# Next pair's rows prepared in DRAM during the second scan, stores spread over the convolution's start, and the quarter-size convolution's loads issued by GpSimd

## The chip, the core and the metric

One core of a Trainium2 chip runs the whole kernel. Its engines are TensorE (PE, with weight loads listed as PEld), VectorE (DVE), ScalarE (ACT), GpSimd (POOL) and SyncE (SP, which here only issues transfers). Each engine works through its own instructions in order; transfers (DMAs) are issued by SP, ACT or POOL and run on 16 shared DMA engines. The metric is device time of one execution in microseconds (us): less is better. The time given for a kernel is the median of its runs.

## The reference

Eight images of 64 channels and 128 x 128 pixels in float32 pass four residual layers, each of which adds its output to its input. Every layer reads a group norm of the image. Cut to what matters:

```python
x = x + relu(batchnorm(deform_conv2d(gn(x), offset, mask, wd)))   # layer 0: 3x3 deformable convolution
x = x + conv3x3(gn(x), weight)                                    # layer 1
v = gn(x)                                                         # layer 2: two state space scans
y_h = s5_block(v.transpose(0, 2, 3, 1), 0)                        #   along rows of the image
y_v = s5_block(v.transpose(0, 3, 2, 1), 1)                        #   along columns
x = x + fusion_w @ concat(y_h, y_v) + fusion_b
v = gn(x)                                                         # layer 3: nearest neighbours
x1 = relu(bn(conv2d(v, wd, stride=4)))                            #   64 x 32 x 32, quarter size
out = mean over the 9 least similar of a 7x7 window(x1) - x1
f = relu(bn(conv3x3(concat(x1, out)))); f = f * sigmoid(bn(wa @ mean(f)))
x = x + bilinear_resize(f, 128, 128)
```

A group norm has 32 groups of two channels and takes its statistics over a whole image, so each layer's first step waits for the last pixel of the layer before. The batch norm of layer 0 takes its statistics over all eight images: its output y is kept in DRAM until all are done, and normalised later.

## The kernel before

**Tiling.** The 128 partitions hold 2 images x 64 channels, a *pair*; four pairs p = 0 to 3 make the batch. A pair is 128 x 16,384 floats, 8 MB.

**Stages.** `deform` makes layer 0 without its batch norm for all pairs and leaves y[p] in DRAM. It takes the first 14.0 ms, and the change does not reach it. `rest` (from L477) does everything else. It owns two *rooms* in SBUF, each as large as a pair: one holds the current pair's image `a`, the other, `b`, holds what the step needs beside it. For each pair:

1. `conv3x3` (layer 1). The statistics of its group norm, `gn1`, come from the routine that made the image. Sixteen times it normalises 8 rows of the image on ACT (nx, L574) and copies them with four transfers on SP into the other room (L576, L577), whose first and middle rows POOL clears first. Then 16 groups of 4 row pairs run: two sets of matmuls (c1, L588), a DVE add onto the image (L590), two DVE statistics (L594).
2. `scan_layer` (layer 2). A first norm fills `b`; then two `Scan` objects, d = 0 along rows and d = 1 along columns. Each goes backward over 16 blocks (`back`, which leaves states in DRAM) and then forward (`ahead`), in steps g. A step of `ahead` has: `inputs` (ACT, fx, L1224, read from `b`; four transfers in<-fx on SP, L1226), `drive` (PE, L1235, then v and u, the sum u on POOL at L1242), `scan` (DVE, L1257), `rebuilt` (one transfer zb<-back on SP, L1280, PE L1282, POOL L1286 and L1288), `outputs` (PE L1302, ACT, DVE L1305), `mixed` (PE L1320, ACT), and `add` of the block before (POOL L1334, PE L1338, DVE add onto the image L1340, and for d = 1 a DVE statistic L1343).
3. The finished image is stored to y[p] with 16 transfers of 512 KB, all issued at once on SP (L504). The room `a` is then the other room for the next pair, and its clearing waits for these stores.
4. `neighbours` (layer 3) is a generator named `aside`. It is not run here: the next pair's `conv3x3` takes one step of it after each set of matmuls, so that layer 3 of pair p lies inside layer 1 of pair p + 1. For the last pair it runs alone at the end. Its first part, `quarter` (L1002), loads weights (L1014), the norm's numbers (L1016) and then, in 8 blocks of 4 transfers each, the image (yq, L1036; from y[p] in DRAM, or from the room for the last pair), all issued by ACT; it runs matmuls pd (L1044) and an activation x1q (L1045). After it come the nine least similar (`farthest`, DVE), their means, a convolution pf (L1112), and the resize, which loads y[p] again (L1135), adds on DVE (L1151, L1152) and stores the output.

**The work around the change.** During the second scan's `ahead`, a generator `following` is stepped once per step g. In the kernel before it does nothing 15 times; at the end, when `b` is no longer needed, it runs `finish_deform` for pair p + 1 into `b`: 16 rows, each a load of x into `b` (L540), a load of y (L542), a batch norm and relu on ACT (L543), an add (L544, on POOL and DVE in turn) and two DVE statistics (L546). Then `gn1` is made from the statistics. y has three buffers in turn, taken from tiles that the scan has finished with.

A scheduler orders the instructions of an engine, within what buffers and data allow; the program's order is therefore not exactly an engine's order.

Of the kernel before, what the change touches and what calls it, by code (L numbers as in the profile page):

```python
# [9 lines left out]
F32 = mybir.dt.float32  # L10
I32 = mybir.dt.int32
AF = mybir.ActivationFunctionType
# [4 lines left out]
P = 128  # L17
# [3 lines left out]
CH = 512  # L21
NCH = HW // CH
# [6 lines left out]
NB = 256  # L29
NG = HW // (T * NB)  # L30

MAT, COS, SIN, ROT, DEC = 0, T * P, T * P + NB + 1, T * P + 2 * NB + 2, T * P + 2 * NB + 2 + P
NSTATE = DEC + 1
# [8 lines left out]
class Net:  # L42
# [434 lines left out]
    def rest(self):  # L477
        tc, nc = self.tc, self.nc
        with ExitStack() as ctx:
            pool = lambda name, bufs, **kw: ctx.enter_context(tc.tile_pool(name=name, bufs=bufs, **kw))  # L480
            self.big = pool("b_big", 1)
            self.small = pool("b_small", 2)
            self.tables = pool("b_tables", 2)
            self.ps = pool("b_ps", 2, space=PSUM)
            self.ps1 = pool("b_ps1", 1, space=PSUM)
            self.back = [[self.dram.tile([P, 2, NB], F32, name=f"back{d}_{g}") for g in range(NG)] for d in range(2)]
            rooms = [self.big.tile([P, ROOM], F32, name=f"room{k}") for k in range(2)]
            image = lambda t: t[:, 0:HW].rearrange("p (h w) -> p h w", h=H)
            aside = iter(())
            with tc.tile_pool(name="b_first", bufs=6) as wp:  # L490
                first = self.finish_deform(0, image(rooms[0]), lambda n: wp.tile([P, 1024], F32, tag="y", name=f"yr0_{n}"))
                for _ in first:
                    pass
            for p in range(self.npair):
                now, other = rooms[p % 2], rooms[(p + 1) % 2]
                a, b = image(now), image(other)
                r, nb = self.conv3x3(p, a, other, *self.gn1, aside)
                norm = self.scan_layer(p, a, b, r, nb)
                af = now[:, 0:HW]

                for n in range(8):
                    for half in range(2):
                        s = slice((half * 8 + n) * 1024, (half * 8 + n + 1) * 1024)
                        nc.sync.dma_start(self.y[p][:, s], af[:, s])  # L504
                aside = self.neighbours(p, self.y[p] if p + 1 < self.npair else af, norm)
            for _ in aside:
                pass

    def setup_deform(self, psum):

# [36 lines left out]
            yield  # L547
        self.gn1 = self.groupnorm(self.small, self.ps1, "small", st, "gn1")

    def conv3x3(self, p, a, room, r, nb, aside):  # L550

        nc, src = self.nc, self.ins["l1_w"]
        st = self.small.tile([P, NCH, 6], F32, tag="st", name=f"gn2_st{p}")
        two = room.rearrange("p (i n w) -> p i n w", i=2, w=H)
        half = [slice(0, C), slice(C, P)]
        with self.tc.tile_pool(name=f"b_conv{p}", bufs=1) as cp, self.tc.tile_pool(name=f"b_conv2_{p}", bufs=2) as wp:

            w = cp.tile([P, 2, 2, 3, C], F32, name=f"l1_w{p}")
            nc.gpsimd.memset(w, 0.0)
            for e in range(2):
                for n in range(2):
                    for h in range(2):
                        dy = 2 * n - 1 + h - e
                        if abs(dy) < 2:
                            nc.scalar.dma_start(w[half[h], e, n], src[:, 3 * dy + 3 : 3 * dy + 6, :])
            nc.gpsimd.memset(two[half[0], :, 0, :], 0.0)
            nc.gpsimd.memset(two[half[1], :, H // 2, :], 0.0)  # L570
            for n in range(16):
                t = wp.tile([P, 2, 4, H], F32, tag="t", name=f"nx{p}_{n}")
                rows = a[:, 8 * n : 8 * n + 8, :].rearrange("p (m e) w -> p e m w", e=2)
                nc.scalar.activation(t, rows, AF.Identity, bias=nb, scale=r)  # L574
                for i in range(2):
                    nc.sync.dma_start(two[half[1], i, 4 * n : 4 * n + 4, :], t[half[i], 0])  # L576
                    nc.sync.dma_start(two[half[0], i, 4 * n + 1 : 4 * n + 5, :], t[half[i], 1])  # L577
            for n in range(0, H // 2, 4):
                for e in range(2):
                    po = self.ps.tile([P, 4, H], F32, tag="b", name=f"c1_{p}_{n}_{e}")  # L580
                    calls = []
                    for dx in (0, -1, 1):
                        c0, c1 = max(0, -dx), min(H, H - dx)
                        for m in range(2):
                            for i in range(2):
                                calls.append((po[half[i], :, c0:c1], w[:, e, m, dx + 1], two[:, i, n + m : n + m + 4, c0 + dx : c1 + dx]))
                    for k, (o, lt, mv) in enumerate(calls):
                        nc.tensor.matmul(o, lhsT=lt, rhs=mv, start=k < 2, stop=k >= len(calls) - 2)  # L588
                    rows = a[:, 2 * n : 2 * n + 8, :].rearrange("p (m e) w -> p e m w", e=2)[:, e]
                    nc.vector.tensor_add(rows, rows, po)  # L590
                    next(aside, None)
                for k in range(2):
                    g = n // 2 + k
                    nc.vector.bn_stats(st[:, g, :], a[:, 4 * g : 4 * g + 4, :].rearrange("p h w -> p (h w)"))  # L594
                next(aside, None)
            for _ in aside:
                pass
        return self.groupnorm(self.small, self.ps1, "small", st, "gn2")
# [319 lines left out]
    def scan_layer(self, p, a, b, r, nb):  # L918

        tc, nc = self.tc, self.nc  # L920
        st = self.small.tile([P, NCH, 6], F32, tag="st", name=f"gn3_st{p}")
        with tc.tile_pool(name=f"b_scan{p}", bufs=2) as wp:
            ways = [Scan(self, wp, p, d, a, b, st) for d in range(2)]

            back = ways[0].back("in", "z", "h")
            for _ in self.first_norm(wp, p, a, b, r, nb):
                next(back)
                next(back)
            for _ in back:
                pass  # L930
            ways[0].ahead(ways[1].back("inb", "zbk", "fx"))

            def following():

                rooms = [(wp, "inb", [P, 2, 2, NB]), (wp, "fx", [P, 2, 2, NB]), (self.tables, "tabs", [P, NSTATE])]

                def room(n):
                    pool, tag, shape = rooms[n % 3]
                    kind = {"bufs": 1} if pool is wp else {}
                    t = pool.tile(shape, F32, tag=tag, name=f"yr{p + 1}_{n}", **kind)  # L940
                    return t[:, 0:1024] if len(shape) == 2 else t.rearrange("p i h m -> p (i h m)")

                for _ in range(NG - 1):
                    yield
                for n, _ in enumerate(self.finish_deform(p + 1, b, room)):
                    if n % 4 == 3:
                        yield

            ways[1].ahead(following() if p + 1 < self.npair else iter(()))

        r, nb = self.groupnorm(self.small, self.ps1, "small", st, "gn3")
        nc.vector.scalar_tensor_tensor(nb, self.bias, r, nb, ALU.mult, ALU.add)
        norm = self.small.tile([P, 2], F32, tag="norm", name=f"norm{p}")
        nc.vector.tensor_copy(norm[:, 0:1], r)
        nc.vector.tensor_copy(norm[:, 1:2], nb)
        return norm
# [45 lines left out]
    def quarter(self, sp, p, src, norm, x1):  # L1002


        nc, S = self.nc, self.S
        half = [slice(0, C), slice(C, P)]
        with self.tc.tile_pool(name=f"b_down{p}", bufs=1) as wp, self.tc.tile_pool(name=f"b_down2_{p}", bufs=3) as yp:
            wd = wp.tile([P, 2, 4, C], F32, name=f"l3_wd{p}")
            taps = self.ins["l3_wd"].rearrange("c (m e g) o -> c e m g o", m=2, e=2)

            norms = wp.tile([P, 2, 2], F32, name=f"norms{p}")
            for e in range(2):
                for m in range(2):
                    nc.scalar.dma_start(wd[half[e], m], taps[:, e, m])  # L1014
                for i in range(2):
                    nc.scalar.dma_start(norms[half[e], i], norm[half[i]])  # L1016
            wd = wd.rearrange("p m g o -> p (m g) o")

            pb = self.ps1.tile([P, 1], F32, tag="small", name=f"pb{p}")
# [11 lines left out]
            for n in range(-2, 8):  # L1031
                if n + 2 < 8:
                    y = yp.tile([P, 2, 8, H], F32, tag="y", name=f"yq{p}_{n + 2}")
                    for e in range(2):
                        for i in range(2):
                            nc.scalar.dma_start(y[half[e], i], rows[half[i], e, 8 * n + 16 : 8 * n + 24, :])  # L1036
                    loaded.append(y)
                if n < 0:
                    continue
# [383 lines left out]
```

## Time and profile before

| what | us |
|---|---|
| median of 4 runs | 18606.06 |
| lowest, highest run | 18596.14, 18632.25 |
| profiled execution, its own time | 18649.83 |
| its span (what the page shows) | 18648.1 |
| PE busy | 11167.3 (60%) |
| DVE busy | 11385.0 (61%) |
| POOL busy | 11000.9 (59%) |
| ACT busy | 3026.1 (16%) |
| start of `rest` in the span | 13,986 |

The page shows one execution. A busy share is a mean over stages with different limits: the deformable stage has 75% of the span. The change is in `rest`, so its stages have to be read one by one, from windows of the trace. The end chain that the page prints covers only the last microseconds and tells nothing of the middle. The mean granted TensorE clock of the execution is 0.76.

In the answers of the trace, a line of a group reads: source line, engine, operation, out<-in, shapes, count | busy us, mean ns of one | idle time of the engine just before them and what ended it. A timeline line reads: start us, length us, engine, line, operation. "SPq" is SP's queue: the time it spends issuing a transfer.

### The profile page before, as it was taken

The page shows a single profiled execution, that of the slowest core. Times are in us where ns is not written, and L with a number is a line of the kernel's source. Part 1 is how long each engine was busy: PE and PEld are TensorE (multiplying, and loading weights), DVE is VectorE, ACT ScalarE, POOL GpSimd, SP SyncE. Part 2 cuts the span into 40 slices and gives each one's busy share as a digit, 9 for nine tenths or more (in the row PEclk, how much of TensorE's full clock was granted, in tenths as well). Part 3 has the DMA queues.
Part 4 walks back from the last instruction along what each step waited for, and adds up shares of the span by engine and source line. Part 5 has one row for each costly group of instructions (what it writes and reads, how often), then busy time and mean ns, then how long its engine had stood idle before and what let it go on. Part 6 is the DMA issues. An engine that isn't in the chain of part 4 may idle for free. (4 is left out here: it accounts for less than half of the span.)

```text
span 18648.1 us, 118301 instructions
## 1 busy us (share of the span) xinstructions
PE 11167.3 (60%) x31224; PEld 3939.1 (21%) x31224; DVE 11385.0 (61%) x27180; ACT 3026.1 (16%) x5658; POOL 11000.9 (59%) x10484
## 2 busy tenths in 40 slices
PE   6555455545555554555645555554427988889886
PEld 1111111111111111111111111111102534435343
DVE  5566666566665566665655665555664765667566
ACT  1000111001100000110000000000003424334242
POOL 5667676676666667666666666666671413315142
PEclk8777677767677676777766766667658999999898
DMA  4333333333333333333333333333333243422433
GB/s 152 101 96 106 115 116 113 109 118 114 115 109 98 97 95 117 116 111 111 100 97 91 97 100 96 97 96 95 89 92 95 68 144 78 129 87 72 140 77 99
DMA packets 900049, 1933.33 MB, mean 104 GB/s; under 512 B 199852, under 2 KB 435764, under 8 KB 876340
## 3 DMA queue, kind: packets, MB, share of 16 engines
q0 software_dynamic: 442368, 1208.55, 22.2%
q1 hardware_dynamic: 381968, 679.49, 12.0%
q10 hardware_dynamic: 75044, 37.72, 1.0%
q8 instruction: 255, 4.18, 0.1%
q14 instruction: 414, 3.39, 0.1%
HBM read 1540.72 MB, written 208.10 MB: 94 GB/s over the span
## 5 line engine op out<-in xcount | busy, mean ns | idle before, releaser
L371 POOL DMA_INDIRECT g<-table,idx x9216 | 9526.6, 1034 | 4321.7 <-issue 2636.6
L381 DVE TENSOR_REDUCE sm<-g 128x64 f32<-128x256 f32 x9216 | 5065.9, 580 | 3567.8 <-remote 2744.1
L289 PE MATMUL po<-xe,wt 128*54 128x512 f32 (+3 forms) x8384 | 4720.6, 673 | 772.3 <-ACT ob L299 545.1
L380 DVE TENSOR_TENSOR g<-g,wts 128x256 f32<-128x256 f32 x9216 | 3558.8, 415 | 562.3 <-DMA g<-table,idx 476.1
L387 PE MATMUL sp<-ident,sm 128*128 128x128 f32 x4096 | 1498.9, 377 | 3483.7 <-DVE sm L381 1833.0
L390 ACT COPY s<-sp 128x512 f32<-128x512 f32 x1024 | 599.1, 585 | 9514.4 <-remote 3935.2
L387 PEld LDWEIGHTS sp<-ident,sm 128*128 128x128 f32 x4096 | 620.5, 155 | 6261.9 <-DVE sm L381 2391.3
L395 PE MATMUL yp<-s,wd 128*64 128x512 f32 (+1 forms) x2560 | 911.5, 719 | 1351.9 <-ACT s L390 733.5
L289 PEld LDWEIGHTS po<-xe,wt 128*54 128x54 f32 x8384 | 922.3, 139 | 2115.7 <-issue 1294.9
L872 POOL COPY l_yb<-ln_y 128x512 f32<-128x512 f32 x128 | 73.1, 615 | 1295.8 <-DVE ln_y L121 1295.8
L588 PE MATMUL c<-room,l_w 128*64 128x508 f32 (+1 forms) x3072 | 740.1, 597 | 21.3 <-DMA room<-nx 15.2
L1242 POOL TENSOR_TENSOR u<-u,v 128x512 f32<-128x512 f32 x256 | 328.5, 1283 | 689.5 <-DVE v L1241 552.7
L1224 ACT ACTIVATE fx<-room,ln_b,ln_g 128x512 f32<-128x512 f32 x512 | 639.2, 1292 | 169.4 <-DMA in<-fx 147.7
L1334 POOL TENSOR_TENSOR ms<-ms,ln_y 128x512 f32<-128x512 f32 x256 | 274.3, 1092 | 638.9 <-DVE ln_y L121 602.7
L389 PE MATMUL s<-ident,sm 128*64 128x128 f32 x1024 | 344.3, 336 | 431.7 <-DVE g L380 110.1
L395 PEld LDWEIGHTS yp<-s,wd 128*64 128x64 f32 (+1 forms) x2560 | 221.0, 158 | 1773.7 <-issue 985.0
L1257 DVE TENSOR_TENSOR_SCAN z<-tabs,z,u 128x256 f32<-128x256 f32 x512 | 434.6, 875 | 215.1 <-POOL u L1242 186.5
L1235 PE MATMUL pv<-in,tabs 128*128 128x512 f32 x1024 | 506.7, 617 | 44.5 <-DVE u L1241 41.2
L396 DVE BATCH_NORM_STATS2 ystat<-yp 128x6 f32<-128x512 f32 x128 | 89.2, 697 | 706.4 <-PE yp L395 413.5
L1320 PE MATMUL pc<-outs,h 128*128 128x256 f32 x2048 | 496.7, 385 | 26.2 <-DVE h L1305 23.9
L1302 PE MATMUL py<-x,outs 128*128 128x512 f32 x1024 | 508.0, 600 | 7.2 <-POOL x L1288 6.8
L1302 PE MATMUL py<-in,outs 128*128 128x512 f32 x1024 | 507.5, 608 | 3.3 <-DMA outs<-out_tab 1.8
(414 smaller groups left out, 10216.7 us busy)
## 6 DMA issues: line engine op xcount, KB each, us to landing
g<-table,idx POOLq DMA_INDIRECT x9216
in<-fx SPq DMA_DIRECT2D x1024, 128.0 KB
xe<-in_x_dram SPq DMA_DIRECT2D x56, 1408.0 KB
table<-q SPq DMA_DIRECT2D x256, 256.0 KB
y<-ys SPq DMA_DIRECT2D x128, 256.0 KB
room<-in_x_dram SPq DMA_DIRECT2D x64, 512.0 KB
yr<-y SPq DMA_DIRECT2D x64, 512.0 KB
room<-nx SPq DMA_DIRECT2D x256, 128.0 KB
```

The source lines that it names most:

```text
L289: nc.tensor.matmul(po[:, r0:r1, c0:c1], lhsT=wt[:, t, :], rhs=xe[:, row + r0 : row + r1, c0 + dx : c1 + dx], start=n == 0, stop=n == len(u ...
L371: nc.gpsimd.indirect_dma_start(out=tq[:, k, :], out_offset=None, in_=flat[i], in_offset=bass.IndirectOffsetOnAxis(ap=idx[:, at : at + 1], ...
L380: nc.vector.tensor_mul(t[:, k], t[:, k], w)
L381: nc.vector.tensor_reduce(sm[:, k], t[:, k].rearrange("p q c -> p c q"), axis=mybir.AxisListType.X, op=ALU.add)
L387: nc.tensor.transpose(sp[:, j, :], sm[:, j * P : (j + 1) * P], self.ident)
L390: nc.scalar.copy(st[i][:, 0:4, m * P : (m + 1) * P], sp)
L395: nc.tensor.matmul(yp[i * C : (i + 1) * C, :], lhsT=wd[0:rows, j, :], rhs=st[i][0:rows, j, :], start=j == 0, stop=j == 4)
L588: nc.tensor.matmul(o, lhsT=lt, rhs=mv, start=k < 2, stop=k >= len(calls) - 2)
L1224: nc.scalar.activation(fx[:, e].rearrange("p h (o m) -> p h o m", m=self.INNER), src[:, e::2], AF.Identity, bias=w["ln1_b"], scale=w["ln1_g"])
L1235: nc.tensor.matmul(pv, lhsT=tabs[:, at : at + P], rhs=fx[:, :, h, :], start=h == 0, stop=h == 1)
L1302: nc.tensor.matmul(py, lhsT=lt, rhs=mv, start=n == 0, stop=n == len(calls) - 1)
L1320: nc.tensor.matmul(pc[:, i], lhsT=hs[:, h, i, m * P : (m + 1) * P], rhs=self.outs[:, CEN : MIX + P], start=True, stop=True)
```

## The change

Three things are changed, all in `rest`.

1. `following` runs a new routine, `prepare_deform`, in the steps that were empty. For each of the 16 rows of pair p + 1 it loads x and y into two SBUF tiles (one buffer each), normalises y on ACT, adds on POOL (always), takes two statistics on DVE, and stores the sum back into y[p + 1] in DRAM. It takes `gn1` from these statistics at once. When `b` is free, eight transfers of 1 MB load the finished image from y[p + 1] into it. The first pair still uses `finish_deform`.
2. The 16 stores of y[p] become a generator, `stores`, of 8 steps with two transfers each. `conv3x3` of the next pair takes two steps before the rooms are cleared and one after every second nx. For the last pair all 16 are issued before `neighbours`, as before.
3. The weight, norm and image loads of `quarter` (40 transfers per pair) are issued by GpSimd instead of ACT.

```diff
@@ rest
-            aside = iter(())
+            aside, stores = iter(()), iter(())
...
-                r, nb = self.conv3x3(p, a, other, *self.gn1, aside)
+                r, nb = self.conv3x3(p, a, other, *self.gn1, stores, aside)
                 norm = self.scan_layer(p, a, b, r, nb)
                 af = now[:, 0:HW]
-
-                for n in range(8):
-                    for half in range(2):
-                        s = slice((half * 8 + n) * 1024, (half * 8 + n + 1) * 1024)
-                        nc.sync.dma_start(self.y[p][:, s], af[:, s])
+                stores = self.stores(p, af)
                 aside = self.neighbours(p, self.y[p] if p + 1 < self.npair else af, norm)
+            for _ in stores:
+                pass
             for _ in aside:
                 pass
+
+    def stores(self, p, af):
+
+        for n in range(8):
+            for half in range(2):
+                s = slice((half * 8 + n) * 1024, (half * 8 + n + 1) * 1024)
+                self.nc.sync.dma_start(self.y[p][:, s], af[:, s])
+            yield
@@ new
+    def prepare_deform(self, p, xr, yr):
+
+        nc = self.nc
+        st = self.small.tile([P, NCH, 6], F32, tag="st", name=f"gn1_st{p}")
+        for n in range(16):
+            s = slice(n * 1024, (n + 1) * 1024)
+            nc.sync.dma_start(xr, self.x[p * P : (p + 1) * P, s])
+            nc.sync.dma_start(yr, self.y[p][:, s])
+            nc.scalar.activation(yr, yr, AF.Relu, bias=self.bn0_bias, scale=self.bn0_scale)
+            nc.gpsimd.tensor_add(xr, xr, yr)
+            for m in range(2):
+                nc.vector.bn_stats(st[:, 2 * n + m, :], xr[:, m * CH : (m + 1) * CH])
+            nc.sync.dma_start(self.y[p][:, s], xr)
+            yield
+        self.gn1 = self.groupnorm(self.small, self.ps1, "small", st, "gn1")
@@ conv3x3
+            for _ in range(2):
+                next(stores, None)
             nc.gpsimd.memset(two[half[0], :, 0, :], 0.0)
             nc.gpsimd.memset(two[half[1], :, H // 2, :], 0.0)
             for n in range(16):
...
+                if n % 2:
+                    next(stores, None)
@@ scan_layer, following
-                rooms = [(wp, "inb", [P, 2, 2, NB]), (wp, "fx", [P, 2, 2, NB]), (self.tables, "tabs", [P, NSTATE])]
...
+                xr = wp.tile([P, 2, 2, NB], F32, tag="inb", name=f"xr{p + 1}", bufs=1).rearrange("p i h m -> p (i h m)")
+                yr = self.tables.tile([P, NSTATE], F32, tag="tabs", name=f"yr{p + 1}")[:, 0:1024]
+                made = self.prepare_deform(p + 1, xr, yr)
                 for _ in range(NG - 1):
+                    next(made, None)
                     yield
-                for n, _ in enumerate(self.finish_deform(p + 1, b, room)):
-                    if n % 4 == 3:
+                for _ in made:
+                    pass
+
+                bf = b.rearrange("p h w -> p (h w)")
+                for n in range(8):
+                    s = slice(n * 2048, (n + 1) * 2048)
+                    nc.sync.dma_start(bf[:, s], self.y[p + 1][:, s])
+                    if n % 3 == 2:
                         yield
@@ quarter
-                    nc.scalar.dma_start(wd[half[e], m], taps[:, e, m])
+                    nc.gpsimd.dma_start(wd[half[e], m], taps[:, e, m])
...
-                    nc.scalar.dma_start(norms[half[e], i], norm[half[i]])
+                    nc.gpsimd.dma_start(norms[half[e], i], norm[half[i]])
...
-                            nc.scalar.dma_start(y[half[e], i], rows[half[i], e, 8 * n + 16 : 8 * n + 24, :])
+                            nc.gpsimd.dma_start(y[half[e], i], rows[half[i], e, 8 * n + 16 : 8 * n + 24, :])
```

More of the change, by code (lines that the diff above doesn't have):

```diff
@@ L548, in finish_deform, with conv3x3 @@
         self.gn1 = self.groupnorm(self.small, self.ps1, "small", st, "gn1")
-    def conv3x3(self, p, a, room, r, nb, aside):
+    def prepare_deform(self, p, xr, yr):
[12 more added lines that the diff above has]
+        self.gn1 = self.groupnorm(self.small, self.ps1, "small", st, "gn1")
+    def conv3x3(self, p, a, room, r, nb, stores, aside):
         nc, src = self.nc, self.ins["l1_w"]
@@ L933, in following @@
             def following():
-                rooms = [(wp, "inb", [P, 2, 2, NB]), (wp, "fx", [P, 2, 2, NB]), (self.tables, "tabs", [P, NSTATE])]
[L937 to L941, printed above, removed]
+                xr = wp.tile([P, 2, 2, NB], F32, tag="inb", name=f"xr{p + 1}", bufs=1).rearrange("p i h m -> p (i h m)")
+                yr = self.tables.tile([P, NSTATE], F32, tag="tabs", name=f"yr{p + 1}")[:, 0:1024]
+                made = self.prepare_deform(p + 1, xr, yr)
                 for _ in range(NG - 1):
+                    next(made, None)
                     yield
-                for n, _ in enumerate(self.finish_deform(p + 1, b, room)):
-                    if n % 4 == 3:
+                for _ in made:
[5 more added lines that the diff above has]
+                    if n % 3 == 2:
                         yield
```

## The prediction

> **What bounds the kernel now.** I read the busy time by slice first: up to 14.0 ms PE, DVE and POOL share the deformable stage, which this change leaves as it is. The last 4,662 us (13,986 to 18,648) hold four pairs, and only there can time move. Next came windows: the second scan's steady stretch of pair 0, then the tail of each pair's second scan, from its last input (L1224) to its last statistic (L1343). Columns: window, length, busy PE, PEld, DVE, ACT, POOL, granted clock, DMA share, GB/s.
>
> ```profile
> 14800.00:14957.10 157.10, 156.96 (x519) 89.35 (x518) 139.75 (x291) 68.98 (x140) 87.85 (x70) 1.00 0.20 50
> 14959.99:15051.50 91.51, 53.01 (x152) 29.52 (x152) 82.18 (x144) 30.81 (x49) 48.17 (x29) 0.78 0.60 201
> 16093.70:16184.60 90.90, 54.33 (x155) 29.93 (x153) 82.58 (x146) 30.96 (x49) 49.08 (x30) 0.76 0.59 200
> 17225.90:17315.60 89.70, 53.27 (x154) 29.47 (x153) 82.72 (x147) 30.84 (x49) 48.56 (x30) 0.77 0.60 202
> 18355.30:18412.30 57.00, 45.21 (x154) 25.85 (x152) 46.03 (x105) 15.07 (x35) 24.15 (x21) 0.90 0.07 18
> ```
>
> The steady scan is PE-bound (156.96 of 157.10), with DVE close behind (13.97 of 15.71 us a step). The tail of pairs 0 to 2 carries the next pair's 16 rows and is DVE-bound; pair 3 has no next pair and shows the bare tail.
>
> ```profile
> L546 DVE BATCH_NORM_STATS2 gn_st<-room 128x6 f32<-128x512 f32 x32 | 21.3, 680 | 2.7 <-POOL room L544 2.7
> L544 POOL TENSOR_TENSOR room<-room,yr 128x1024 f32<-128x1024 f32 x8 | 19.4, 2429 | 14.1 <-ACT yr L543 12.5 <-DMA room<-in_x_dram 1.6
> L543 ACT ACTIVATE yr<-yr,bn_bias,bn_scale 128x1024 f32<-128x1024 f32 x14 | 17.4, 1245 | 11.6 <-DMA yr<-y 11.5
> L544 DVE TENSOR_TENSOR room<-room,yr 128x1024 f32<-128x1024 f32 x8 | 12.5, 1566 | 0.0
> ```
>
> These groups of the first tail are the rows: 33.8 us of DVE explain 82.18 against 46.03. Then SP's timeline in the steady steps (start, length, instruction):
>
> ```profile
> 14921.65 0.33 SPq L1280 DMA_DIRECT2D zb<-back  x1
> 14923.19 2.38 SPq L1226 DMA_DIRECT2D in<-fx  x4
> 14937.37 0.33 SPq L1280 DMA_DIRECT2D zb<-back  x1
> 14938.91 2.38 SPq L1226 DMA_DIRECT2D in<-fx  x4
> 14953.08 0.33 SPq L1280 DMA_DIRECT2D zb<-back  x1
> 14954.63 3.50 SPq L1226 DMA_DIRECT2D in<-fx  x4
> ```
>
> A step is 15.71 us and SP must issue four in<-fx in each. The last set goes at 14954.63 and the matmul that reads it, L1235, starts at 14960.02 after 0.32 us of waiting for it: there is no spare time behind these loads. Last, the waits of the stage after, conv of pair 1 with pair 0's quarter convolution:
>
> ```profile
> DVE room L590 <- PE c L588: 100.5, 17, 35.9
> ...
> ACT nx L574 <- DMA room<-nx: 41.6, 12, 7.9
> ...
> ACT x1q L1045 <- DMA yq<-y: 25.4, 1, 25.4
> ACT nx L574 <- DVE gn_nb L149: 21.4, 1, 21.4
> ```
>
> With T = 15,048 (last add, L1340): the stores go at 15,048.96, gn1 is ready at 15,057.2, ACT issues twelve yq from 15,061.97 for 23.06 us between two nx, the first c1 starts at T+42.
>
> **Part 1: rows out of the tail.** The tail falls from a mean of 90.70 to 57.00: **-33.7 us** a pair, three times. Below 57 it can't go: the last steps' own chain sets that, as in pair 3.
>
> **Part 2: rows into the scan.** In the built order of the changed program SP holds, between the in<-fx of one step and of the next, one or two rows of: store (waits for POOL's add), yr load, xr load (waits until that store has landed, xr being single). Sixteen rows fall in nine steps: seven of two, two of one. Steps of before: 9 x 15.71 = 141. Length of one row, r:
> - Store, issue to landing. The nearest row is nx's 128 KB, 2.47 us (pair 0: last issue at 14,042.63, ACT released at 14,045.10). A further 384 KB at 366 GB/s (the window of 15,050 to 15,060, when y's stores run) is 1.1: 3.5 (an estimate). The yr load beside it, another 512 KB or 1.4: up to 5.0. I take 4.2.
> - xr load, alone: 3.5. POOL add 2.35 (L544's undisturbed instances; the mean is 2.43, the longest 3.16). Issue of the second DMA 0.35. Waiting in POOL's queue, busy 8.8 of 15.7 us a step already: 0 to 0.8, I take 0.4.
> So r = 10.8, from 9.6 to 12.0. SP runs in order, so in<-fx stands behind both rows: from the xr issued just before one in<-fx to that before the next lie two whole rows, and a step with two lasts 2r. After a one-row step, xr and the add have already run while SP waited, and it is 3.9 (in and zb issues) + (r - 6.25: without 3.5 + 2.35 + 0.4) + r. A one-row step stays 15.71. Sum: 5 x 21.6 + 2 x 19.25 + 2 x 15.71 = 178, **+37 us** a pair; 161 (+20) at 9.6, 195 (+53) at 12.0. The other queues follow in the same time: PE waits at L1235, and everything behind it in PE's order, scan and outputs, with it. DVE gets two statistics (2 x 0.68) per row and, in a two-row step, needs 13.97 + 2.7 = 16.7 of 21; POOL 8.8 + 4.9; ACT 6.9 + 2.5: these are covered by the longer step, and without it DVE alone would need 13.97 + 16 x 1.36 / 9 = 16.4 a step, 6 us over nine.
>
> The Trainium skill ("SBUF — State Buffer", section "Who interferes with whom") says that a DVE instruction with two SBUF inputs and a GpSimd one that reads SBUF exclude each other for a whole instruction, which speaks against adds on POOL alone. The trace leans the same way: at 14,970.00, beside a POOL add (14,969.92, 2.34 us), two scans of L1257 took 4.41 us on DVE, against a mean of 0.875 each. By the rule, 16 x 2.35 = 38 us would be taken from DVE where such instructions meet; spread over nine steps that is 4.2 each, and the two-row step would be near 21 on DVE too, so not a second price but the same one.
>
> **Part 3: b filled by eight 1 MB loads.** 8 MB at 366 GB/s is 23 us and lies in the bare tail of 57, whose DMA share is 0.07. Three of them stand on SP ahead of the last in<-fx, which shares its engines with them: 0 to 8 (3 x 2.9), I take **+3**.
>
> **Part 4: stores in conv, gn1 early, quarter off ACT.** Conv starts sooner: two store steps instead of eight, no gn1 wait, no yq between nx. Memsets wait about 5 us for stores (15,048.96 to 15,053.99 before), nx and room<-nx take 5: first c1 at about T+11, not T+42. But DVE's chain ends the stage. Before: last pd at T+105, then x1 18, farthest 70, means and pf 17, to up 25, up 60, next stage 8: 304, as measured. In the built order the eighth pd moves from behind c1_12_1 to behind c1_24_1: 11 + 6.75 groups x 10.94 (conv of pair 0: 175 us for 16 groups) + 8 pd x 4 = T+117, 12 later; gn2's chain, now inside up, gives back 7. **+5 us** a pair. Bounds: -30 (the earlier start is kept: pd does not hold the chain) to +15.
>
> **Part 5: 40 loads per pair issued by POOL.** Before shows no plain POOL load; the nearest row is
>
> ```profile
> L371 POOL DMA_INDIRECT g<-table,idx x9216 | 9526.6, 1034 | 4321.7 <-issue 2636.6
> ```
>
> with 128 pieces of data an instruction; a yq load has 64 x 8 rows of 512 B, so 0.95 (its median) to 4 x 0.95 = 3.8. I take 2.1, nearer the row, since the row is the only instance of a POOL issue. In conv, four of 2.1 are 8.4 against 10.94 per group: hidden by PE. At the end of the program nothing hides them:
>
> ```profile
> 18412.70:18484.00 71.30, 40.53 (x299) 28.63 (x299) 5.45 (x27) 3.67 (x8) 0.00 (x0) 0.75 0.96 235
> ```
>
> Here the 16 DMA engines are at 0.96, so a cheaper issue gains nothing: 40 x 2.1 = 84 against 71, **+13**, from 0 to 152 - 71 = +81. The skill ("SBUF — State Buffer", section "SBUF: two separate sides") warns that DVE can keep GpSimd from writing descriptors, and gives 3,100 ns where one takes 620 alone. By that figure 40 would be 124, an estimate of +53; but DVE is busy 5.45 of 71.3 us here.
>
> **Sum**: 3 x (-33.7 + 37 + 3 + 5) + 13 = **+47**. The profiled execution took 18,649.8 (span 18,648.1 and 1.7 outside), so 18,697 by its own time; that execution lies 43.8 above the median of 18,606, against which I forecast **18,653**.
>
> **Rivals.**
> - *The rows fit* (faster): if r is at its lower end, 9.6, they cost 20, and if conv keeps 20 of its 31 us, 3 x (-33.7 + 20 + 3 - 20) = -92 and the quarter 0: **18,514**. For it: DVE and POOL have room, DMA share is 0.20. Against: in<-fx behind the rows, and DVE's up chain. With the rest as taken, the sign turns at rows of 21 us, r = 9.7.
> - *A draw*: rows 28 (r = 10.2), conv -5, quarter 0: 3 x (-7.7) = -23, **18,583**. Same mechanism, smaller rows.
> - *POOL's issue is the bound*: at 3.8 a yq block takes 15.2, more than a conv group (the point where it decides is 10.94/4 = 2.7). Then pd ends 15 later, 3 x (11.3 + 15) + 81 = +160, **18,766**. For it: 512 pieces per load. Against: L371's 1.03 mean with DVE busy 61%.
> - *The scheduler leaves the rows in the tail*: excluded by the built order.
>
> **Numbers.** Forecast 0.48, the rows fit 0.24, draw 0.18, POOL's issue 0.10. The forecast's own range is 18,610 to 18,710 (rows 28 to 46, quarter 0 to 35). About 0.2%, 37 us, can be told from no change. Slower: 0.40 of the forecast and POOL's 0.10, 0.50; within: 0.08 and 0.16, 0.24; faster: 0.24 and 0.02, 0.26. For 8 in 10 the range reaches down to the better part of the first rival and up short of the third: 18,530 to 18,745.
>
> **What would show it.** Tails of 57 to 62 us in pairs 0 to 2; second-scan steps of 19 to 22 us alternating with 15.7, with PE waiting at L1235's matmul for in<-fx, SP at the store and at xr; first c1 near T+11 but the next stage near T+304 to 310; POOL issue rows of about 2 us. Wrong if the steps stay at 15.7 (rows free), if the tail keeps 90, if c1's earlier start reaches the next stage, or if x1q waits for yq in every group.

## The result and the profile after

The changed kernel takes 18,666.89 us (median of 49 runs) against 18,608.46 us (75 runs): ratio 1.0026, with a 95% interval of 1.0018 to 1.0035, so about 48 us slower (the two medians lie 58 apart). The forecast was +47. Its sum came out, but not all of its terms, and the reason given for the largest of them fell.

The profiled execution of the changed kernel has a span of 18,686.4 us, 38.3 more than before. To see where they lie I cut the span into stages at marks that every kernel has: a *scan stage* runs from a pair's first centring matmul (L902 before, L928 after) to the last statistic of its second scan (L1343, L1371), a *convolution stage* from there to the next pair's first centring matmul, and the *last stage* from pair 3's last statistic to the end.

| stage, us | before | after |
|---|---|---|
| up to the first centring matmul | 14,219.6 | 14,203.7 |
| scan stage, pairs 0, 1, 2 | 831.4, 831.7, 826.9 | 854.5, 851.0, 848.4 |
| scan stage, pair 3 (prepares no rows) | 793.7 | 791.8 |
| of it: after the end of the last input, pairs 0 to 3 | 88.6, 88.4, 87.1, 54.6 | 57.8, 58.4, 58.3, 54.2 |
| convolution stage, three times | 301.9, 304.0, 303.0 | 302.4, 301.7, 301.4 |
| last stage | 235.8 | 231.5 |

From the first centring matmul on, the kernel is 54.3 us longer (4,482.7 against 4,428.4); the 15.9 us less before it are in work that the change does not reach and differ from run to run. The loss is in three scan stages, 19 to 23 us each. Their tails did shrink by 30, so the steps before the tail got longer by about 50.

Windows of the changed kernel (columns as before): eight steps of pair 0's forward second scan, all with rows, three tails, and the quarter convolution of the last pair.

```profile
14759.94:14929.65 169.71, 143.12 (x419) 79.24 (x418) 133.19 (x257) 68.98 (x129) 100.19 (x69) 0.92 0.52 155
...
15000.40:15058.20 57.80, 42.70 (x147) 24.35 (x145) 46.24 (x110) 13.72 (x35) 24.46 (x23) 0.90 0.45 170
16153.30:16211.70 58.40, 43.21 (x151) 24.87 (x149) 47.23 (x116) 13.79 (x34) 24.49 (x23) 0.91 0.44 169
17303.50:17361.80 58.30, 43.18 (x151) 24.84 (x149) 47.19 (x114) 13.79 (x34) 24.43 (x23) 0.91 0.45 169
...
18455.00:18523.60 68.60, 38.75 (x299) 28.91 (x299) 5.92 (x27) 3.20 (x7) 25.97 (x39) 0.71 0.88 247
```

Eight steps take 169.71 us, 21.2 each instead of 15.71. No engine is full in them: PE 143 of 170, DVE 133, POOL 100. PE went from 156.96 of 157.10 to 84%: it now waits. The question is for whom. One such step on SP (timeline: start, length, instruction):

```profile
14821.88 2.39 SPq L1254 DMA_DIRECT2D in<-fx  x4
14824.37 0.52 SPq L1308 DMA_DIRECT2D zb<-back  x1
14827.12 0.33 SPq L568 DMA_DIRECT2D y<-xr  x1
14827.50 0.42 SPq L563 DMA_DIRECT2D yr<-y  x1
14830.02 0.33 SPq L562 DMA_DIRECT2D xr<-in_x_dram  x1
14838.75 0.32 SPq L568 DMA_DIRECT2D y<-xr  x1
14839.16 0.38 SPq L563 DMA_DIRECT2D yr<-y  x1
14841.89 0.33 SPq L562 DMA_DIRECT2D xr<-in_x_dram  x1
14843.19 2.39 SPq L1254 DMA_DIRECT2D in<-fx  x4
```

That is the picture of the forecast: two rows of store, yr, xr between two sets of in<-fx, 21.3 us, each xr about 3 us behind its store (2.90 and 3.14). But the other steps do not fit it. Over the eight, the stores of two rows stand 12.6 us apart in the mean; five steps hold two stores and take 19.3 to 23.8 us, three hold one and take 20.7 to 21.5. The last of the eight (from 14,908.12) holds one store and no load of a row, and still takes 21.5. Pairs 1 and 2 show the same (19.3 to 24.0 and 20.8 to 21.7). The waits of the eight steps (total, times, longest) speak against the reading that rows on SP make the step, too. SP's queue first, then the engines:

```profile
SPq L568 <- POOL xr L565: 54.1, 10, 8.9
SPq L562 <- DMA y<-xr: 21.5, 10, 2.3
SPq L1254 <- DVE h L1333: 14.3, 8, 3.0
```

```profile
ACT yr L564 <- DMA yr<-y: 21.8, 9, 6.1
PEld pc L1348 <- DVE h L1333: 19.9, 7, 4.4
PE pc L1348 <- DVE h L1333: 18.4, 8, 3.6
...
DVE gn_st L567 <- POOL xr L565: 11.0, 8, 2.0
```

SP is through with its rows and then still waits, eight times, for DVE's h (14.3 us in all) before it may issue in<-fx, as it did in the kernel before (10.8 us in ten steps). PE's wait is for h too. It starts the matmul that reads in<-fx (L1263) 4.5 to 8.1 us after their issue, and a wait for them is not in the list (in pair 1's steps there are 0.9 us of it). And DVE, which makes h, stands 11 us at the rows' statistics until POOL's add is done; ACT stands 21.8 us at the rows' relu until yr has landed. So a second theory had to be tested against mine.

### The profile page after: what moved, and what is told of

Same layout as the page of the kernel before. It is cut to its first block, busy times and chain, and to the rows that moved or that the text cites. A ratio compares the mean times of both kernels' runs of the same rounds, so it can differ in the third digit from the quotient of the medians.

```text
span 18686.4 us, 118530 instructions
## 1 busy us (share of the span) xinstructions
PE 11190.5 (60%) x31224; PEld 3951.8 (21%) x31224; DVE 11370.3 (61%) x27156; ACT 3022.6 (16%) x5658; POOL 11146.6 (60%) x10668
## 5 line engine op out<-in xcount | busy, mean ns | idle before, releaser
L1263 PE MATMUL pv<-in,tabs 128*128 128x512 f32 x1024 | 508.6, 619 | 49.9 <-DVE u L1269 39.4
```

The costliest lines, as they stand in the source:

```text
L1263: nc.tensor.matmul(pv, lhsT=tabs[:, at : at + P], rhs=fx[:, :, h, :], start=h == 0, stop=h == 1)
```

## The experiments

**Theory A** (the prediction's): in<-fx stands behind two whole rows in SP's order. **Theory D**: the rows' compute stands in the in-order queues of POOL, DVE and ACT, between instructions of a loop that has no spare time. **Rival B**: the loss is made in the convolution. Each run's stages are in one table at the end of this section. The chips differ by up to 250 us, and one by 2,200, in what lies ahead of the first scan stage, so stages are compared, and ratios only with the kernel before on the same chip. Five runs without a ratio below (in_on_act, rows_no_dma, rows_dma_only, rows_dve, rows_act_dve) are single executions. Pair 3's scan stage, which prepares no rows, lies between 786 and 798 us over all kernels but in_on_act, so a difference of some 10 us between the stages of two runs says little.

**One part at a time.** In each kernel the other two parts are put back to what they were.

```diff
 rows_only:    part 1 (prepare_deform in the scan, b from DRAM)
 stores_only:  part 2 (stores in steps)
 quarter_only: part 3 (nc.gpsimd.dma_start in quarter)
```

> Only part 1 of the change: the rows prepared in DRAM during the second scan; the 16 stores at once and the quarter's loads on ACT as before. Theory A (the rows inside the scan are what costs): per pair 0 to 2 the scan stage, from the first matmul of the centring step to the last statistic, goes from 831 to about 851 us and its tail after the last input from 88 to about 58, as in the changed kernel; the convolution stage stays within 5 us of 302; in all +55 to +65, about 18,668 us, ratio 1.003. Rival B (the loss is made in the convolution, by the spread stores or by POOL's loads): the scan stage gains nothing or little, ratio 1.000 or under.

> Only part 2: the 16 stores of y in steps, inside the next convolution. Theory A: scan stages stay at 831, 832, 827, 794 us; the convolution stage stays at 302 within 5 us, because the eight matmul groups of the quarter convolution stand further back in PE's order and DVE's chain behind them ends the stage; ratio 0.999 to 1.001. Rival B: convolution stage longer by 10 us or more, ratio over 1.0015. Rival C (the earlier start is kept): stage shorter by 20 to 30 us, ratio 0.996.

> Only part 3: the quarter's 40 loads per pair issued by POOL. The changed kernel shows 0.68 us an issue. Theory A: scan stages unchanged, convolution stage 302 within 5 us, the last stage (after the last scan, 235.8 us before) shorter by 0 to 6 us; ratio 0.999 to 1.001. Rival B: convolution stage longer by 10 us or more.

Ratios 1.0030 (1.0015 to 1.0046), 1.0004 (0.9988 to 1.0019) and 0.9999 (0.9982 to 1.0015). Rows alone have the scan stages of the changed kernel, 843 to 852 us; the other two leave them at 826 to 832. The spread stores alone make the convolution stage 305 to 308; with gn1 early as well (the changed kernel) it is 301 to 302. POOL's loads change nothing. Rival B is out: the loss is part 1's.

**One row per step.** A tiny ACT copy ties the load of y to the step's layer norm.

```diff
+            if way.done is not None:
+                nc.scalar.copy(yr[:, 0:1], way.done[:, 0:1])
             nc.sync.dma_start(yr, self.y[p][:, s])
```

> The changed kernel, with each row's load of y held back by one tiny ACT copy that needs that step's layer norm: the built order then has one row per step instead of two. Theory A (SP's order: in<-fx stands behind two whole rows of store, y load, x load, each about 10 to 11 us): a step with one row fits into 15.7 us, steps of the second scan fall from 20.4 to 23.8 back to 15.7 to 17, the scan stage from 851 to 800 to 815 us per pair, in all about 18,560 us, ratio 0.995 to 0.998. Rival D (the rows' work in the queues of POOL, ACT and DVE costs, wherever it lies): the same 16 rows cost the same, about 3 us each, scan stage about 850 us, ratio 1.002 to 1.004.

Ratio 1.0065 (1.0043 to 1.0087), scan stages 874 to 878 us: worse. One row per step, and from in<-fx to in<-fx these steps still take 20.0 to 21.7 us. Theory A's central number, that one row fits into 15.7, is refuted. Theory D's 850 us was missed as well: spread over more steps, the same rows cost more. The timeline of one step (POOL, ACT, PE, DVE, then SP; the bracket is the idle time before and who ended it):

```profile
15073.25 2.35 POOL L567 TENSOR_TENSOR xr<-xr,yr 128x1024 f32<-128x1024 f32 x1
15075.56 1.26 POOL L1318 TENSOR_TENSOR x<-x,xt 128x512 f32<-128x512 f32 x1
...
15077.60 0.38 ACT L1351 ACTIVATE qs<-pc 128x256 f32<-128x256 f32 x1 [4.49 <-DVE var L1354]
...
15080.49 0.96 PE L1368 MATMUL tp<-ident,ms 128*128 128x128 f32 x4 [3.10 <-DVE ln_ve L111]
...
15082.95 2.43 PE L1265 MATMUL pv<-in,tabs 128*128 128x512 f32 x4
...
15075.63 1.28 DVE L569 BATCH_NORM_STATS2 gn_st<-xr 128x6 f32<-128x512 f32 x2 [2.87 <-POOL xr L567]
15076.84 0.67 DVE L1354 TENSOR_REDUCE var<-qs 128x8 f32<-128x512 f32 x1
...
15075.63 0.32 SPq L570 DMA_DIRECT2D y<-xr  x1
15076.04 2.49 SPq L1256 DMA_DIRECT2D in<-fx  x4
```

POOL adds a row; DVE has the row's statistics next and idles 2.87 us for that add, then takes 1.28 for them. Only then comes the reduction L1354 that ACT has waited 4.49 us for, ACT's output leads to the layer norm L111, and PE waits 3.10 us for that. 2.87 + 1.28 = 4.15 of the 5.2 us by which this step of 20.9 is longer. This kernel's SP also issues in<-fx only behind a store that waits for the same add (15,076.04), but PE reaches the matmul that needs it at 15,082.95, some 7 us later and without a wait for it (L1265).

**Taking each queue out.** Each edit is against the changed kernel.

```diff
 rows_no_dma:   transfers only for the first row's loads and the last row's store
 rows_dma_only: relu, add and statistics only for the last row
 rows_dve:      -nc.gpsimd.tensor_add(xr, xr, yr)   +nc.vector.tensor_add(xr, xr, yr)
 rows_act_dve:  as rows_dve, and statistics as two ACT passes with accum_out
 in_on_act:     -nc.sync.dma_start(out[...], fx[...])   +nc.scalar.dma_start   (forward, d = 1)
```

> The changed kernel with the forward second scan's in<-fx issued by ACT instead of SP, so that they stand behind no row on SP. Theory A: steps of 15.7 to 17, scan stage 805 to 820 us. Theory D: scan stage within 8 of 851. Pair 3, which prepares no rows, shows what the issue on ACT costs by itself: 792 us, give or take 5.

> The changed kernel with the rows' 48 transfers per pair left out, except those of the first load and the last store: ACT's relu, POOL's add and DVE's two statistics run 16 times on what lies in the two tiles, so the rows of pairs 1 to 3 and their statistics are not the reference's. Theory A (in<-fx stands behind the rows' transfers on SP): nothing is left for SP to hold, the steps of the second scan return to 15.7 to 16.5 us and the scan stage of pairs 0 to 2 from 851 to 800 to 812 us. Theory D (the rows' work in the queues of DVE and POOL: statistics that wait for POOL's add, POOL's own operations behind that add, and DVE operations that a POOL add stretches): the work is all there, scan stage 835 to 855.

> The counterpart of the run without transfers: the changed kernel with all the rows' transfers, and with relu, add and statistics left out but for the last row, so that the rows of pairs 1 to 3 are x without the batch-normed y and their statistics are not the reference's. The run without transfers had scan stages of 831 to 839 us, against 850 for the changed kernel and 800 for bare rows (831 less a tail shorter by 31). If the two parts add up, transfers alone give 810 to 820. If SP's order alone made the step (theory A), store and loads without an add between are 7 us a row, two rows fit under 15.7, and the stage is at 800 to 808. 840 or more would mean that the transfers are the cost after all and the compute part was a coincidence.

> The changed kernel with the rows' adds on DVE instead of POOL. DVE gets 16 x 1.2 us more, but waits for no add of POOL and is not stretched by one. Theory D: the waits (11 us of statistics for POOL's add in eight steps of the changed kernel) and the stretch (scans of 1.49 us instead of 0.88, 16 of them) go, the scan stage falls to 825 to 842 us. Theory A: the row's chain is 1.2 us shorter of 10.8, two rows 2.4 per step: about 830 to 840 too, so this run alone does not tell A from D; a stage of 850 or more speaks against D.

> The changed kernel with nothing of the rows on POOL and less on DVE: the add on DVE (1.2 us a row), the statistics as two ACT passes with accumulated sums (2 x 1.24 us a row) instead of two DVE ones (1.36). Theory D (the queues of DVE and POOL set the row's price): the price falls again, from 50 us for POOL adds and 37 for DVE adds to 15 to 25, scan stage 815 to 826 us for pairs 0 to 2. Rival (any work put into an in-order queue of this loop costs, ACT's too, since PE waits for h and ACT stands before h): scan stage 835 to 850, no better than with DVE's statistics.

With in<-fx on ACT no transfer of a row stands before it (the row's relu does, in ACT's order), and the scan stages are 879 to 889; both theories had said less, since pair 3, without rows, is 822 itself: the price on ACT of the issue, 31 us, was not foreseen at all (5 were allowed). Mean of pairs 0 to 2 less pair 3: 61.3, against 59.5 in the changed kernel. Of the 61.3, some 7 us are a wait of PE for in<-fx in the tail, which the changed kernel does not have; without the tails the rows cost 49.2 us here and 55.5 there. Theory A's numbers left some 13 to 28 (805 to 820 against 792), so SP's order before in<-fx makes little of the price. Where the steps with two rows are steady (five of pair 0, 120.7 us instead of five times 18.0), DVE stands 29.5 us at the statistics waiting for POOL's add, about what these steps are longer by (30.7).

Against 800 us for a scan without the rows' cost (831 less a tail shorter by 31), compute without transfers costs 31 to 39 (831 to 839, at the foot of D's range or just under it), transfers without compute 6 to 14 (806 to 814), together 37 to 53, against the 48 to 55 of the changed kernel. Two reservations: without transfers to wait for, the scheduler put the sixteen adds 3.8 to 13.3 us apart, in 82 us around the start of the forward second scan; and ACT stood 46.6 us, in thirteen times, at the relu there until POOL's add had let go of yr, where the changed kernel waits for yr's load. So this run weighs the compute, but not at its old place. Adds on DVE take 14 us off (834 to 840), which is in D's range but was in A's too; moving the statistics to ACT as well takes off nothing (837 to 841), where D had said 815 to 826: the rival of that run was right. So taking load off DVE is not enough. That foreign work costs by its place in any of these queues, ACT's included, fits all these runs; none of them isolates it queue by queue.

**Why the earlier convolution start gained nothing.** In the changed kernel c1 starts 14 us after the last add (15,056.9 to 15,070.6; 42 before), and the next stage still begins at the same distance from that add, 304 us.

```diff
-                if n % 2:
-                    next(stores, None)
+                if n < 3:
+                    next(stores, None)
+                    next(stores, None)
+                if 1 < n < 11:
+                    next(aside, None)
```

> The changed kernel with the stores of y all issued during the first three nx (two steps of stores up front, then two more after each) and one step of the aside taken after each of nx 2 to 10, so that the quarter convolution's matmul groups stand earlier in PE's order: the eighth behind c1_12_1 instead of c1_24_1, pf behind c1_36_1 instead of c1_48_0. If the earlier start of the convolution was given back because these groups stood late and DVE's chain behind them ends the stage: the convolution stage of 301 to 302 us falls to 265 to 285, three times, in all -50 to -110 against the changed kernel, ratio 0.997 to 1.000 to the kernel before. If another resource holds the stage (the 16 DMA engines, or PE's 257 us of work): 295 or more, ratio 1.002 to 1.003.

Ratio 1.0008 (0.9989 to 1.0026); convolution stages 291.8, 292.9, 295.0. The quarter convolution ends 17 to 19 us earlier against the stage's start than in the changed kernel in the first two, but only 6 to 11 reach the end; 17 to 37 were expected. Windows of early3 after that show why:

```profile
15420.00:15440.00 20.00, 20.00 (x87) 8.12 (x83) 15.40 (x47) 2.73 (x6) 0.00 (x0) 1.00 0.01 1
15440.00:15460.00 20.00, 20.00 (x101) 9.31 (x101) 16.07 (x47) 3.50 (x10) 0.00 (x0) 1.00 0.00 1
15460.00:15480.00 20.00, 19.38 (x96) 8.65 (x97) 18.02 (x52) 3.57 (x10) 0.00 (x0) 1.00 0.00 1
```

PE is full in these windows (59.4 of 60 us); over the whole stage it is busy 258.9 of 291.8. So behind DVE's chain stood PE's work, some 10 us away. Both stated ranges were missed: the stage is between 285 and 295 in two pairs of three.

**A place with room.** The last two kernels take early3 and put the rows into the convolution's groups of the pair before, one per group, with two buffers each from tiles that are idle there; the second scan keeps only the eight 1 MB loads.

```diff
+            made = self.prepare_deform(p + 1, wp) if p + 1 < self.npair else iter(())
             for n in range(0, H // 2, 4):
...
+                next(made, None)
```

> The rows of the next pair prepared a stage earlier: inside the convolution's groups of the pair before (one row per group, adds on DVE, two buffers each from tiles that are idle there), with the early stores and early aside of the run early3; the second scan keeps only the eight 1 MB loads. If the rows are dear in the scan because its loop leaves no queue a gap, and cheap where PE alone holds the stage: scan stages of pairs 0 to 2 at 797 to 805 us (831 before), convolution stages 293 to 305, the last stage 231; in all 70 to 100 us under the kernel before, ratio 0.9946 to 0.9962. If the rows cost what they cost wherever they are (16 x 2.5 us of DVE, 40 us), convolution stages of 325 to 335 and ratio 0.999 to 1.000.

> The same with the rows' adds on POOL, which is nearly idle in the convolution (27 of 302 us). If the statistics' wait for POOL's add and the stretch of DVE beside it matter there too (DVE's resize is busy 10 of 10 us): convolution stages longer than with DVE's adds by 5 to 20 us each. If POOL's idle time is worth more than that: shorter by up to 10.

conv_two, with adds on DVE: ratio 0.9957 (0.9938 to 0.9976), 18,724.09 against 18,809.14 us on that chip. conv_two_pool: 0.9969 (0.9949 to 0.9989). Of the kernels that leave no work out, these two are the only ones that beat the kernel before, and their intervals overlap, so it is the stages that tell them apart. The scan stages are 786 to 799 us in both, as pair 3's within the spread above. conv_two's ratio came as forecast, by two misses that cancel: its scan stages are up to 11 us below the 797 to 805 that were expected, its convolution stages with rows (313.2, 316.5) up to 12 above the 293 to 305. The rows' price there is read against the stage of pair 3, which prepares none (294.2 and 294.9): 19 to 22 us with DVE's adds, 39 to 41 with POOL's (17 and 22 more, where 5 to 20 were expected). Pair 0's groups, where the first rows lie, take 175 us in conv_two instead of 167. The rows' lines in one such stage of conv_two, then of conv_two_pool:

```profile
L569 DVE BATCH_NORM_STATS2 gn_st<-xr 128x6 f32<-128x512 f32 x32 | 21.6, 697 | 0.2
L567 DVE TENSOR_TENSOR xr<-xr,yr 128x1024 f32<-128x1024 f32 x16 | 19.7, 1236 | 14.3 <-ACT yr L566 5.9 <-ACT feat L1143 5.5 <-issue 2.0
```

```profile
L567 POOL TENSOR_TENSOR xr<-xr,yr 128x1024 f32<-128x1024 f32 x16 | 43.9, 2744 | 158.7 <-DMA xr<-in_x_dram 95.2 <-ACT yr L566 41.3 <-DVE ninth L1207 11.7
L569 DVE BATCH_NORM_STATS2 gn_st<-xr 128x6 f32<-128x512 f32 x32 | 20.9, 680 | 23.9 <-POOL xr L567 23.9
```

With POOL's adds DVE stands 23.9 us before the statistics; with its own, 0.2. That wait is more than the 19.7 us that the adds cost DVE.

| kernel | scan stage, pairs 0, 1, 2 | pair 3 | convolution stages | last |
|---|---|---|---|---|
| rows_only | 850.7, 851.5, 843.2 | 794.4 | 301.7, 301.3, 301.2 | 234.9 |
| stores_only | 831.1, 826.4, 826.5 | 792.0 | 307.0, 305.1, 308.1 | 234.9 |
| quarter_only | 831.8, 829.0, 830.0 | 786.1 | 302.4, 303.2, 301.2 | 233.3 |
| rows_paced | 878.3, 874.9, 874.2 | 785.9 | 302.6, 300.7, 299.7 | 231.3 |
| in_on_act | 889.1, 879.0, 882.9 | 822.4 | 300.6, 301.4, 301.8 | 232.1 |
| rows_no_dma | 839.0, 830.9, 834.7 | 796.9 | 302.7, 301.4, 302.0 | 230.5 |
| rows_dma_only | 813.6, 806.0, 806.6 | 791.9 | 302.0, 301.1, 300.2 | 231.4 |
| rows_dve | 840.3, 838.3, 833.7 | 797.8 | 302.0, 302.6, 300.7 | 226.9 |
| rows_act_dve | 841.3, 836.7, 838.5 | 796.1 | 302.0, 301.4, 301.0 | 231.8 |
| early3 | 853.3, 843.3, 842.8 | 788.9 | 291.8, 292.9, 295.0 | 230.2 |
| conv_two | 796.9, 786.0, 787.5 | 787.1 | 316.5, 313.2, 294.2 | 230.5 |
| conv_two_pool | 788.5, 798.8, 787.1 | 789.4 | 333.8, 335.6, 294.9 | 230.4 |

## Why the prediction was right, and where it was not

- **The sum**, +47, against 0.0026 x 18,606 = +48. By the stages it is 54. It came out by luck: three errors mostly cancelled, rows 14 us a pair too cheap (+42), the convolution 6 a pair too dear (-18), the last quarter 17 too dear.
- **Part 1**, -33.7 a pair: the tail's bare length by pair 3 is 54.2 to 54.6, from 88.0: -33.6. Right.
- **Part 3**, the 1 MB loads, +3: the tails of pairs 0 to 2 are 3.6 to 4.2 us longer than pair 3's 54.2. The number fits, the reason probably does not: in conv_two the same eight loads go out at the same place and the tails are 53.7 to 53.9, no longer than its pair 3's 55.1. What the changed kernel's tail has besides them is gn1's norm; no run takes that out alone.
- **Part 2**, rows in the scan, +37 from +20 to +53: measured, scan stage +21.3 in the mean and 29.9 from the tail, +51. This is the step that failed, in size and more in its reason. Its length of a row was too short: 12.6 us from store to store, against 10.8 and 12.0 at most (the least terms add up to 9.7, not 9.6). Store to xr was about as taken (2.9 to 5.8 us where no in<-fx lay between, 4.2 forecast), but from xr to the next store it took 8.1 in the mean and not 6.25, with SP waiting 54 us in ten times for POOL's add. Steps with two rows did take about 2r = 21.6, but steps with one row took as long, so that this fitted was a coincidence. And in<-fx was not late: SP waits for h after the rows, PE waits for in<-fx in none of the eight steps, in<-fx freed from the rows' transfers gains some 6 us of 55, and in rows_paced one row a step costs as much as two. The sentence that dismissed DVE and POOL ("these are covered by the longer step", "6 us over nine") added up busy time, 16.4 us of DVE a step, and left out that a queue in order also passes on its waits: in eight steps 11 us of DVE at the statistics and 21.8 of ACT at the relu. Its own table had warned: DVE had 1.7 us to spare a step and PE none. A quantity that fits two mechanisms (some 21 us a step) was put down to the one that had been worked out.
- The **Trainium skill's rule** weighed there ("SBUF — State Buffer", section "Who interferes with whom") is seen in the changed kernel; two timelines, DVE and POOL:

```profile
14836.45 2.82 DVE L1285 TENSOR_TENSOR_SCAN z<-tabs,z,u 128x256 f32<-128x256 f32 x1
...
14839.26 0.74 DVE L1285 TENSOR_TENSOR_SCAN z<-tabs,z,u 128x256 f32<-128x256 f32 x1
...
14836.38 2.34 POOL L565 TENSOR_TENSOR xr<-xr,yr 128x1024 f32<-128x1024 f32 x1
```

The first of two equal scans starts 0.07 us after a POOL add and ends 0.55 after it: it stood still for nearly the whole add. Over the eight steps, though, a scan takes 1.49 us in the mean against 1.23 in the steady steps before (not 0.88, the mean of the program, which the prediction and an expectation above compare with): 16 x 0.26 = 4 us, where the prediction had 38 by the rule. Exclusion is seen here, and is a small part of the 51.
- **Part 4**, +5 (from -30 to +15): measured +0.5, -2.3, -1.6. The mechanism held to a few microseconds: c1 at T+14 (forecast T+11), the eighth group done at T+120 (T+117), next stage at T+304. That the groups' place in PE's order was the only thing in the way did not hold: early3 gained 6 to 11, not 30.
- **Part 5**, +13 from 0 to +81: measured -4.3 for the whole last stage. The issue is 0.68 us, below the lower bound of 0.95 taken from the indirect DMA. Group by source line in the changed kernel (min/median/max ns):

```profile
L1064 POOL DMA_DIRECT2D yq<-y x96: 682/684/910, 15067.3 to 17456.3; - x96
L1064 POOL DMA_DIRECT2D yq<-room x32: 682/682/722, 18455.1 to 18512.0; - x32
```

A row of another kind of instruction was no bound. That a cheaper issue gains little there, with the DMA engines at 0.96 (now 0.88), fits: the stretch went from 71.3 to 68.6 us. The rule cited for this part (same page, section "SBUF: two separate sides", descriptors held up by DVE, which the page says of DVE's 2-port modes) shows at most as 0.91 us among these 96, with DVE busy 156 us of 302.
- Of the **rivals**, "the rows fit" and "a draw" failed at rows of 51 us, "POOL's issue is the bound" at 0.68 us.

What stays open: how the 51 us divide between waits for POOL's add, the stretch beside it, and ACT's part, its wait for yr above all. The runs show that the rows' work in the scan costs and that SP's order before in<-fx does not make most of the price, not a sum that closes; bn_stats moved away from the add, with the add left on POOL, was not tried.

## What to carry to other kernels

Work added to a loop whose limiting engine is full can cost more than its busy time, as here, where each engine took its instructions in order and handed its wait on: count where the foreign instruction stands and whom it waits for, and put its parts on one engine if you can (a statistic behind its own engine's add waited 0.2 us, behind another's 23.9). When a step gets longer, ask of each queue's last wait before the critical instruction whether it still waits for someone else; if so, that queue is not the cause, however full it looks. And before paying to squeeze work into the tightest stage, look for one with idle engines: the same rows cost 51 us in the scan and 20 in the convolution.

## What the runs showed of the hardware

A plain load issued by POOL, 64 partitions x 8 rows of 512 B, took 0.68 us of POOL's time, with or without crowded DMA engines. The same load issued by ACT in the kernel before took 0.58 us in the median from DRAM, and 1.22 from the room with the DMA engines at 0.96; the last four blocks of four there took ACT 4.1 to 5.2 us each. Issuing in<-fx from ACT instead of SP cost some 30 us over one scan (pair 3: 822 against 792 in the changed kernel; steps of 18.0 instead of 15.7), though ACT was busy only 6.9 of 15.7 us a step. Where nothing else held it, the load behind a 512 KB store was issued 2.9 to 3.3 us after the store, with the yr load of another 512 KB beside it: below both ends (3.5 and 5.0) of the prediction's estimate.
